# Row copies on SyncE in place of one gather in every eighth chunk of a two-layer relational graph convolution

## The chip, the core and the metric

The kernel runs on one core of a Trainium2 chip. The metric is the device time of one execution in microseconds; the median of three runs is given for the kernel before. Profiles come from one separate execution. PE is TensorE, DVE VectorE, ACT ScalarE, POOL GpSimd and SP SyncE.

## What is computed

There are 50000 nodes with 128 features each and 850000 edges with a source `src`, a target `dst` (sorted) and one of 16 types. The last 50000 edges before sorting are self loops. Cut to what matters:

```python
def layer(h, src, dst, rel, basis, w_comp, loop_w, bias):
    W = einsum('rb,bio->rio', w_comp, basis)              # 16 types from 8 bases
    seg = dst * 16 + rel
    agg = segment_sum(h[src], seg, 50000 * 16).reshape(50000, 16, 128)
    return relu(einsum('nri,rio->no', agg, W) + h @ loop_w + bias)
h = layer(x, ...first weights...)
h = layer(h, ...second weights...)
out = layernorm(x + h)
```

All data are float32. For each edge the row `h[src]` has to be fetched: some 800000 rows of 512 bytes in each layer, since self loops are handled apart.

## The kernel before

**Set-up.** While layer 1 runs, the edge lists are read, self loops are taken out, and the remaining 800000 edges are laid out in 6250 tiles of 128 edges. `rows_of` (L438) puts the source numbers of a tile into a column of `src`, one number on each of 128 partitions, clamped to N - 1. This work is a generator, `later_rows` (L845), of which the chunk loop takes one step per chunk, and more where a chunk would need rows that aren't ready yet.

**Chunks.** A layer is a loop over C = 625 chunks (L940) of K = 10 tiles. For every tile, `gather` (L200 to L204) has POOL issue one indirect transfer: 128 rows of 512 bytes, each from the node that `src` names, into one slot of a ring of GATHERS = 5 buffers of ten slots, fifty in all. The gathers of chunk c + 2 stand in the program at chunk c (L947 to L950). A gather may start when PE has used what was in its slot five chunks ago. Then, for each tile, PE multiplies the gathered rows with `hot`, a matrix of weights and zeros that DVE makes (L869, L876), into `pa` (L974). After five tiles ACT copies `pa` into `aT` (L982). Once per four chunks PE multiplies `aT` by the eight bases (L746), ACT copies the result (L752), PE turns it (L756), and DVE spreads it over slots (L734). PE adds the slots to node sums in `pn` (L788). Beside this run the nodes' own terms (`from_itself`: load of `h_own` L677, L687, L691, eight matmuls and products L702 and L709 and a sum L717 for each group), and `finish` (L805), which adds and stores the result, with a normalisation in layer 2.

**Order.** `beside` (L915) writes by hand which piece of the side work follows which tile. PE, POOL, DVE and ACT keep this order (`manual_schedule`, L861). SP isn't in that list: the order of its transfers is left to the framework's planner. SP issues the loads of edge types `rel` (L617, one for four chunks), `lrel` (L644), `h_own`, `xw` (L787) and the stores (L813, L818). Each engine's queue is in order: an instruction that waits holds up those behind it. Transfers from SP are announced on eight completion lanes that are used in turn, and a transfer is issued only when the one before it on its lane has landed.

**Between the layers.** Layer 2 gathers from H1, which layer 1 writes, so its first gather waits for the last store. `count_up` (L537) then decides whether the assumptions held; if not, `summed` computes everything in another way. With these inputs it is skipped.

Of the kernel before, what the change touches and what calls it, by code (L numbers as in the profile page):

```python
# [39 lines left out]
F32 = mybir.dt.float32  # L40
I32 = mybir.dt.int32
BF16 = mybir.dt.bfloat16
U8 = mybir.dt.uint8
U16 = mybir.dt.uint16
AF = mybir.ActivationFunctionType
OP = mybir.AluOpType
# [4 lines left out]
P = 128  # L51
EPR = 850000
ROW = 10
WN = 12
K = P // WN
S = K * WN
RUN = 672
HALF = K // 2
LIVE = HALF * P
BITS = 6  # L60
LK = 64
LBITS = 10
FETCH = 2
AT = 8
PER = 5
Q = AT // 2
BANK = 512
WEIGHTS = AT * PER * 8
BITS_AT_ONCE = BANK - WEIGHTS - WN
GATHERS = 5  # L70
J = 4
NEAR = 128
BATCH = 4
LAG = BATCH + 2
EPS = 1e-5

# [6 lines left out]
def tile_rgcn_resnorm(  # L83
# [15 lines left out]
    nc = tc.nc  # L99
    N, D = x.shape  # L100
    NR, NB = w_comp1.shape
    E = edges.shape[1] // 3
    R, M = -(-E // RUN), E - N
    C = -(-M // (K * P))
    NG = -(-R // P)
# [3 lines left out]
    ROWS = list(range(0, 2 * C, P)) if 2 * C <= P else [0, *range(P - 8, 2 * C, P)]  # L109
# [4 lines left out]
        end = min(2 * C, ROWS[j + 1] if j + 1 < len(ROWS) else 2 * C) * LIVE  # L114
        return min(NG - 1, -(-(end + LIVE) * E // (M * RUN * P)) - 1) if j else 0

    assert D == P and N >= P and edges.shape[0] == 1 and AT * NR == P and PER * NB * WN <= BANK and AT * PER * NB == WEIGHTS and PER == HALF and S <= P and C >= 4 and M > 0 and N % C == 0 and N % J == 0 and J * D == BANK and C % BATCH == 1 and C > 4 * BATCH and RUN - LK // 2 == LIVE and 2 * C <= NG * P and N <= 1 << 16 and E % ROW == 0
    full, rest = divmod(N, P)
    U = divisor(full, 15)
    assert E < 1 << 24 and 2 * N < 1 << 24  # L120
# [4 lines left out]
    FULL = dram.tile([2 * NP, 2], F32, name="FULL")  # L125

    REL = dram.tile([2 * C, LIVE], U8, name="REL")
    NL = -(-(N + LK) // GN) * GN
    LREL = dram.tile([2 * NL, 1], I32, name="LREL")

# [70 lines left out]
    def gather(to, of, idx):  # L201
        return nc.gpsimd.indirect_dma_start(  # L202
            out=to, out_offset=None, in_=of, in_offset=bass.IndirectOffsetOnAxis(ap=idx, axis=0)
        )  # L204
# [233 lines left out]
    def rows_of(j, pool):  # L438
# [33 lines left out]

        placed = put(srcf, src)

        begin = pool.tile([P, HALF], F32, name="begin")
        tiles = halves[:m, :, 0].rearrange("p (k e) -> p k e", e=P)
        nc.vector.tensor_copy(begin[:m], tiles[:, :, 0])
# [58 lines left out]

    def count_up(pool):  # L537
        last = 5 * NG + len(ROWS)
        off = pool.tile([1, C], F32, name="off_all")
        even = pool.tile([1, C], F32, name="even")  # L540
        nc.gpsimd.iota(
            even,
            pattern=[[N // C, C]],
            base=0,
            channel_multiplier=0,
            allow_small_or_imprecise_dtypes=True,
        )
        nc.vector.tensor_tensor(off, first_of, even, op=OP.subtract)
        for i, (most, op) in enumerate(((-NEAR, OP.is_ge), (NEAR, OP.is_le))):
            nc.vector.scalar_tensor_tensor(  # L550
                even,
                off,
                float(most),
                ones[0:1, 0:1].to_broadcast([1, C]),
                op0=op,
                op1=OP.mult,
                accum_out=picked[0:1, last + i : last + i + 1],
            )
        pick = pool.tile([P, 2], F32, name="pick")
        nc.vector.tensor_reduce(pick[:, 0:1], squares, AX.X, OP.add)  # L560
        nc.vector.tensor_reduce(pick[:, 1:2], picked, AX.X, OP.add)
        total = ps_o.tile([P, BANK], F32, name="po")
        nc.tensor.matmul(total[:1, :2], ones[:, 0:1], pick, start=True, stop=True)
        off = pool.tile([1, 2], F32, name="off2")
        nc.vector.tensor_scalar(off[:, 0:1], total[:1, 0:1], float(N), None, op0=OP.not_equal)
        nc.vector.tensor_scalar(
            off[:, 1:2], total[:1, 1:2], float(E + 2 * NG * (P + 1) + 2 * C), None, op0=OP.not_equal
        )
        nc.vector.tensor_tensor(bad, off[:, 0:1], off[:, 1:2], op=OP.max)
# [19 lines left out]
    def chunked():  # L589
        with (  # L590
# [5 lines left out]
            def ks(c):  # L596
                return min(K, -(-M // P) - c * K)
# [223 lines left out]
            def done(steps):  # L821
                for _ in steps:
                    pass

            loaded, stored = [0], [1]
            rest_of_set_up = set_up(pr)
            next(rest_of_set_up)
# [34 lines left out]
            for n, of in enumerate((x, H1)):  # L862
# [33 lines left out]
                def own_of_all():  # L896

                    for g in range(NGR):
                        while now[0] < min(first(g) + LAG - 5, C - LAG - 2):
                            yield  # L900
                        if n == 0 and g % T == 0:
                            end = min(N, (g + T) * GN)
                            while stored[0] < min(NG, -(-(end + NEAR) * E // (N * RUN * P))):
                                next(coming)
                            loaded[0] = end
                        yield from from_itself(g, of, n)
                        made[0] = g + 1
# [28 lines left out]
                weigh = weights(0, n)  # L936
                next(weigh)
                now, made = [0], [0]
                owning = own_of_all()
                for c in range(C):  # L940
                    now[0] = c
                    if n == 0 and c:

                        next(coming, None)
                        while ready[0] + 1 < len(ROWS) and 2 * min(C, c + FETCH + 5) > ROWS[ready[0] + 1]:
                            next(coming)
                    for to in range(0 if c == 0 else c + FETCH, min(C, c + FETCH + 1)):  # L947
                        buffer = (n * C + to) % GATHERS
                        for k in range(ks(to)):
                            gather(rows[buffer][:, k, :], of, src[:, to * K + k : to * K + k + 1])  # L950
                    g = rows[(n * C + c) % GATHERS]
                    if c == 0:
                        pm = next(weigh)
                        hots[0] = hot_of(0, pm)
                        hots[1] = hot_of(1, pm)
                        if n == 0:
                            done(first_runs)
                    hot = hots.pop(c)
                    if c % BATCH == 0:
                        aTs[c // BATCH] = hp.tile([P, NB, BATCH * S], F32, name="aT")  # L960
                    aT, place_of = aTs[c // BATCH], c % BATCH * S
                    if c >= ALONE + 2:
                        if c == ALONE + 2:
                            done(summing)
                        summing = sum_up(c - 2)
                    elif c % BATCH == 0:
                        summing = slots_of_batch(c - BATCH, aTs[c // BATCH - 1], st, n) if c else iter(())
                    for k in range(0, K, PER):
                        m = min(PER, ks(c) - k)
                        if m > 0:  # L970
                            pa = ps_a.tile([P, BANK], F32, name="pa")
                        for i in range(PER):
                            if i < m:
                                nc.tensor.matmul(  # L974
                                    pa[:, i * NB * WN : (i + 1) * NB * WN],
                                    g[:, k + i, :],
                                    hot[:, k + i].rearrange("e b w -> e (b w)"),
                                    start=True,
                                    stop=True,
                                )  # L980
                            if i == m - 1:
                                nc.scalar.copy(  # L982
                                    aT[:, :, place_of + k * WN : place_of + (k + m) * WN].rearrange(
                                        "d b (i w) -> d i b w", w=WN
                                    ),
                                    pa[:, : m * NB * WN].rearrange("d (i b w) -> d i b w", i=m, w=WN),
                                )
                            beside(k + i, c, owning, summing)
                    if c + 2 < C:
                        if (c + 2) % Q == 0:  # L990
                            pm = next(weigh)
                        hots[c + 2] = hot_of(c + 2, pm)
                        if c + 3 < C and (c + 3) % Q == 0:
                            weigh = weights(c + 3, n)
                            next(weigh)
                    for one in added_in(c + 1) if c + 1 < C else ():
                        masks[one] = masks_of(one)
                    if n == 0 and c == 3:
                        beginning.close()
                    if n == 0 and c == C - 1:  # L1000
                        done(coming)
                        count_up(pr)
# [199 lines left out]
```

## Time and profile before

| | |
|---|---|
| median of 3 runs | 18612.61 us (18609.55 to 18622.79) |
| profiled execution, own time | 18435.78 us |
| its span | 18434.0 us |
| mean granted TensorE clock | 0.762 |
| PE matmuls busy | 11416.0 us (62%) |
| POOL busy | 11894.1 us (65%), 12500 gathers |
| DVE busy | 6704.1 us (36%) |
| ACT busy | 1926.2 us (10%) |
| SP transfers issued | 1000 |
| moved | 1044.31 MB, mean 57 GB/s |

An engine's busy share is the time in which its instructions run, not counting waits and the issuing of transfers on SP. In a group's row, the first figures are its busy time and the mean of one instruction in ns; behind the bar stands how long the engine was idle just before these instructions, and what ended most of that idle time. "issue" means that the profile shows nothing it waited for, and "remote" that the end of the wait isn't on record. A share of busy time averages over stages; what a change is worth has to be read in the stage that it touches.

### The profile page before, as it was taken

The page shows a single profiled execution, that of the slowest core. Times are in us where ns is not written, and L with a number is a line of the kernel's source. Part 1 is how long each engine was busy: PE and PEld are TensorE (multiplying, and loading weights), DVE is VectorE, ACT ScalarE, POOL GpSimd, SP SyncE. Part 2 cuts the span into 40 slices and gives each one's busy share as a digit, 9 for nine tenths or more (in the row PEclk, how much of TensorE's full clock was granted, in tenths as well). Part 3 has the DMA queues.
Part 4 walks back from the last instruction along what each step waited for, and adds up shares of the span by engine and source line. Part 5 has one row for each costly group of instructions (what it writes and reads, how often), then busy time and mean ns, then how long its engine had stood idle before and what let it go on. Part 6 is the DMA issues. An engine that isn't in the chain of part 4 may idle for free. (4 is left out here: it accounts for less than half of the span.)

```text
span 18434.0 us, 136664 instructions
## 1 busy us (share of the span) xinstructions
PE 11416.0 (62%) x45072; PEld 7482.7 (41%) x45072; DVE 6704.1 (36%) x11496; ACT 1926.2 (10%) x3706; POOL 11894.1 (65%) x12533
## 2 busy tenths in 40 slices
PE   4565555656566666666656666666666666666666
PEld 3343333434344444444444444444444444444444
DVE  4344344444333333333333333333333333333333
ACT  0010000101000000010101111111111111111111
POOL 5666666666666666666656666666666666666665
PEclk8777777777777777777777777777777777777777
DMA  2222222222122122221212222222222222222221
GB/s 70 62 60 58 56 58 60 61 59 60 53 54 55 54 54 54 54 54 54 55 49 57 57 57 57 57 57 57 57 57 58 57 57 57 57 57 57 57 57 51
DMA packets 540034, 1044.31 MB, mean 57 GB/s; under 512 B 214689, under 2 KB 259011, under 8 KB 539319
## 3 DMA queue, kind: packets, MB, share of 16 engines
q0 software_dynamic: 403552, 826.82, 17.1%
q1 hardware_dynamic: 132551, 207.21, 3.5%
q8 instruction: 364, 5.96, 0.1%
q14 instruction: 351, 2.88, 0.0%
q10 hardware_dynamic: 3216, 1.45, 0.0%
HBM read 962.30 MB, written 72.31 MB: 56 GB/s over the span
## 5 line engine op out<-in xcount | busy, mean ns | idle before, releaser
L202 POOL DMA_INDIRECT g<-H,src x6250 | 5929.8, 949 | 3090.0 <-issue 1304.3
L202 POOL DMA_INDIRECT g<-in_x_dram,src x6250 | 5938.3, 950 | 3029.0 <-issue 1267.5
L974 PEld LDWEIGHTS pa<-hot,g 128*128 128x128 f32 x25000 | 4547.2, 229 | 6044.9 <-issue 5010.2
L974 PE MATMUL pa<-hot,g 128*128 128x96 f32 x25000 | 4581.9, 308 | 3009.5 <-issue 2081.6
L746 PE MATMUL ps<-aT,basis 128*128 128x480 f32 x4960 | 2910.5, 672 | 707.7 <-ACT aT L982 476.2
L982 ACT COPY aT<-pa 128x480 f32<-128x480 f32 x2500 | 1388.0, 558 | 15113.3 <-remote 8194.1
L788 PE MATMUL pn<-slots,own 120*128 120x512 f32 x4128 | 2553.4, 741 | 615.4 <-DVE slots L734 289.2
L702 PE MATMUL po<-basis,hT 128*128 128x512 f32 x3136 | 2048.6, 741 | 1319.1 <-DVE by L709 1101.2
L709 DVE TENSOR_TENSOR by<-po,lw 128x512 f32<-128x512 f32 x1568 | 1069.5, 687 | 4167.5 <-remote 1469.1
L876 DVE TENSOR_TENSOR hot<-fixed,own 128x960 f32<-128x960 f32 x1250 | 1447.1, 1158 | 2091.2 <-remote 1580.7
L734 DVE TENSOR_TENSOR slots<-po,which 120x512 f32<-120x512 f32 x1240 | 782.6, 683 | 2747.6 <-remote 933.8
L717 DVE TENSOR_REDUCE ls<-by 128x128 f32<-128x1152 f32 (+1 forms) x784 | 1664.2, 2123 | 34.1
L788 PEld LDWEIGHTS pn<-slots,own 120*128 120x128 f32 x4128 | 865.5, 238 | 1202.2 <-issue 687.4
L746 PEld LDWEIGHTS ps<-aT,basis 128*128 128x128 f32 x4960 | 879.1, 221 | 754.3 <-ACT aT L982 494.9
L702 PEld LDWEIGHTS po<-basis,hT 128*128 128x128 f32 x3136 | 563.8, 225 | 1390.6 <-DVE by L709 1151.7
L869 DVE TENSOR_TENSOR own<-fixed,key 128x120 bf16<-128x120 f32 x1250 | 344.5, 276 | 2106.3 <-remote 1040.9
L756 PE MATMUL po<-ident,by_slot 128*120 128x128 f32 x1240 | 317.9, 348 | 1129.2 <-ACT by_slot L752 742.8
L756 PEld LDWEIGHTS po<-ident,by_slot 128*120 128x120 f32 x1240 | 178.3, 181 | 1171.5 <-ACT by_slot L752 770.4
L771 DVE TENSOR_SCALAR own<-col,node 120x128 f32<-120x128 f32 x2064 | 529.4, 296 | 10.4 <-PE pn L788 10.4
L629 PE MATMUL fixed<-each,is_rel 128*128 128x64 f32 x3140 | 457.2, 300 | 8.4 <-DVE is_rel L624 6.1
L629 PEld LDWEIGHTS fixed<-each,is_rel 128*128 128x128 f32 x3140 | 444.1, 221 | 9.4 <-DVE is_rel L624 7.3
L798 PEld LDWEIGHTS pn<-loop,hT 128*128 128x128 f32 x1568 | 234.5, 213 | 134.0 <-issue 133.6
(137 smaller groups left out, 2892.7 us busy)
## 6 DMA issues: line engine op xcount, KB each, us to landing
g<-in_x_dram,src POOLq DMA_INDIRECT x6250
g<-H,src POOLq DMA_INDIRECT x6250
rel<-REL SPq DMA_DIRECT2D x312, 80.0 KB
h_own<-in_x_dram SPq DMA_DIRECT2D x97, 256.0 KB
xw<-in_x_dram SPq DMA_DIRECT2D x97, 256.0 KB
H<-ls SPq DMA_DIRECT2D x97, 256.0 KB
h_own<-H SPq DMA_DIRECT2D x97, 256.0 KB
out_dram<-ls SPq DMA_DIRECT2D x97, 256.0 KB
```

Source lines behind the costliest of these rows:

```text
L202: return nc.gpsimd.indirect_dma_start(out=to, out_offset=None, in_=of, in_offset=bass.IndirectOffsetOnAxis(ap=idx, axis=0))
L629: nc.tensor.matmul(of[:, :, j * NB : (j + 1) * NB], is_rel[:m, j * P : (j + 1) * P], EACH[n][:m], start=True, stop=True,)
L702: nc.tensor.matmul(hb[:m], hT[:, j, :m], BASIS[n][:, b : b + few, :].rearrange("p b d -> p (b d)"), start=True, stop=True,)
L709: nc.vector.tensor_tensor(by[:m, b : b + few, :], hb[:m].rearrange("p (b d) -> p b d", d=D), lw[:m, j, g % T, b : b + few, None].to_broadc ...
L717: nc.vector.tensor_reduce(ls[:m, j, :], by[:m].rearrange("p b d -> p d b"), AX.X, OP.add)
L734: nc.vector.tensor_tensor(st[:k], of[:k, None, :].to_broadcast([k, J, D]), which[:k, c, :, None].to_broadcast([k, J, D]), op=OP.mult,)
L746: nc.tensor.matmul(ps[:, : BATCH * S], BASIS[n][:, b, :], aT[:, b, :], start=b == 0, stop=b == NB - 1)
L771: nc.vector.tensor_scalar(own[:k], col4[:k], node4[:k, c : c + 1], float(-g * GN), op0=OP.subtract, op1=OP.is_equal)
L788: nc.tensor.matmul(sums[g], own, of[:k].rearrange("s j d -> s (j d)"), start=c == first(g), stop=c == final(g),)
L876: nc.vector.tensor_tensor(hot[:, : ks(c)], pm[:, c % Q * K : c % Q * K + ks(c), :, None].to_broadcast([P, ks(c), NB, WN]), own[:, : ks(c), ...
L974: nc.tensor.matmul(pa[:, i * NB * WN : (i + 1) * NB * WN], g[:, k + i, :], hot[:, k + i].rearrange("e b w -> e (b w)"), start=True, stop=True,
L982: nc.scalar.copy(aT[:, :, place_of + k * WN : place_of + (k + m) * WN].rearrange("d b (i w) -> d i b w", w=WN), pa[:, : m * NB * WN].rearr ...
```

## The change

In each layer, chunks 15, 23, 31, ..., 623 get only nine gathers. The tenth tile of such a chunk is brought by SP, row by row: 128 transfers of 512 bytes, each with its address from a register. The registers are loaded, 32 at a time, from a new array ROW_AT in device memory, into which `rows_of` now writes the byte offsets (source number times 512) of the last 128 edges of each half chunk. The rows land in a tile `by_hand` of its own (two buffers) instead of the ring.

The copies for chunk c begin at chunk c - 11 and are spread evenly over the first nine tile steps of eight chunks, so the last is handed out at chunk c - 4. `issue_after` keeps the loads of registers behind the last copy issued. Because offsets are needed earlier, the loop asks for set-up rows eleven chunks sooner. To make room, `count_up` uses two tiles of the set-up in place of its own. ACT copies no rows.

```diff
+BY_HAND = 8
+EARLY = 3
+OFFSETS = 32
...
+    ROW_AT = dram.tile([2 * C, P], I32, name="ROW_AT")
...
+        row_at = pool.tile([P, LIVE], F32, name="real").bitcast(I32)[:, :P]
+        nc.vector.tensor_scalar(row_at[:m], srcf[:m, LIVE - P :], float(N - 1), float(4 * D), op0=OP.min, op1=OP.mult)
+        nc.sync.dma_start(ROW_AT[r0 : r0 + m], row_at[:m])
...
-        off = pool.tile([1, C], F32, name="off_all")
-        even = pool.tile([1, C], F32, name="even")
+        off = pool.tile([P, RUN], F32, name="k_f")[0:1, :C]
+        even = pool.tile([P, RUN], F32, name="loop_f")[0:1, :C]
...
+            def by_hand(c):
+                return ks(c) == K and c >= BY_HAND + EARLY and c % BY_HAND == BY_HAND - 1
+            def row_by_row(c, of):
+                row_at = hp.tile([1, P], I32, name="row_at")
+                nc.sync.dma_start(row_at, ROW_AT[2 * c + 1 : 2 * c + 2])
+                to = hp.tile([P, D], F32, name="by_hand")
+                byte = of.bitcast(U8).rearrange("n d -> (n d)")
+                yield to
+                steps = BY_HAND * (K - 1)
+                for step in range(steps):
+                    for e in range(step * P // steps, (step + 1) * P // steps):
+                        if e % OFFSETS == 0:
+                            with tc.issue_after(behind[-1]) if behind else ExitStack():
+                                _, offsets = nc.values_load_multi_w_load_instructions(
+                                    row_at[:, e : e + OFFSETS],
+                                    engines=[mybir.EngineType.SP],
...
+                        row = to.bitcast(U8)[e : e + 1, :]
+                        behind[:] = [nc.sync.dma_start(row, byte[None, ds(offsets[e % OFFSETS], 4 * D)]).ins]
+                    yield to
...
-                        while ready[0] + 1 < len(ROWS) and 2 * min(C, c + FETCH + 5) > ROWS[ready[0] + 1]:
+                        while ready[0] + 1 < len(ROWS) and 2 * min(C, c + FETCH + 5 + BY_HAND + EARLY) > ROWS[ready[0] + 1]:
...
-                        for k in range(ks(to)):
+                        for k in range(ks(to) - by_hand(to)):
                             gather(rows[buffer][:, k, :], of, src[:, to * K + k : to * K + k + 1])
+                    to = c + BY_HAND + EARLY
+                    if to < C and by_hand(to):
+                        fetching = row_by_row(to, of)
+                        handed[to] = next(fetching)
...
-                                    g[:, k + i, :],
+                                    g[:, k + i, :] if k + i < ks(c) - by_hand(c) else handed.pop(c),
...
+                            if k + i < K - 1:
+                                next(fetching, None)
```

More of the change, by code (lines that the diff above doesn't have):

```diff
@@ L115, in needed @@
         return min(NG - 1, -(-(end + LIVE) * E // (M * RUN * P)) - 1) if j else 0
-    assert D == P and N >= P and edges.shape[0] == 1 and AT * NR == P and PER * NB * WN <= BANK and AT * PER * NB == WEIGHTS and PER == HALF and S <= P and C >= 4 and M > 0 and N % C == 0 and N % J == 0 and J * D == BANK and C % BATCH == 1 and C > 4 * BATCH and RUN - LK // 2 == LIVE and 2 * C <= NG * P and N <= 1 << 16 and E % ROW == 0
+    assert D == P and N >= P and edges.shape[0] == 1 and AT * NR == P and PER * NB * WN <= BANK and AT * PER * NB == WEIGHTS and PER == HALF and S <= P and C >= 4 and M > 0 and N % C == 0 and N % J == 0 and J * D == BANK and C % BATCH == 1 and C > 4 * BATCH and RUN - LK // 2 == LIVE and C <= RUN and 2 * C <= NG * P and N <= 1 << 16 and E % ROW == 0
     full, rest = divmod(N, P)
@@ L823, in done @@
                     pass
+            behind = []
+            def by_hand(c):
[14 more added lines that the diff above has]
+                                    engines=[mybir.EngineType.SP],
+                                    min_val=0,
+                                    max_val=(N - 1) * 4 * D,
+                                    skip_runtime_bounds_check_because="sources are clamped to N - 1, and none is below 0",
+                                )
+                        row = to.bitcast(U8)[e : e + 1, :]
+                        behind[:] = [nc.sync.dma_start(row, byte[None, ds(offsets[e % OFFSETS], 4 * D)]).ins]
+                    yield to
             loaded, stored = [0], [1]
@@ L938, in chunked @@
                 now, made = [0], [0]
+                handed, fetching = {}, iter(())
                 owning = own_of_all()
```

## The prediction, made before the result was known

> **What bounds the kernel now.** I read the page's costliest groups first, then a table by stretches, then a timeline of one stretch. The groups (busy, mean ns | idle before):
>
> ```profile
> L202 POOL DMA_INDIRECT g<-H,src x6250 | 5929.8, 949 | 3090.0 <-issue 1304.3
> L202 POOL DMA_INDIRECT g<-in_x_dram,src x6250 | 5938.3, 950 | 3029.0 <-issue 1267.5
> ...
> L974 PE MATMUL pa<-hot,g 128*128 128x96 f32 x25000 | 4581.9, 308 | 3009.5 <-issue 2081.6
> ```
>
> No engine is full: PE is busy 62% of the span, POOL 65%. A gather is 0.95 us busy, and one that waits for nothing starts 0.30 us after the one before: 1.25 us each, 12.5 us for a chunk of ten. The table shows the real pace (time, POOL busy with number of gathers, granted clock, DMA share, GB/s):
>
> ```profile
> 7000.00:9000.00 2000.00, 1322.59 (x1396) 0.77 0.20 54
> 10000.00:12000.00 2000.00, 1320.61 (x1393) 0.76 0.21 57
> 14000.00:16000.00 2000.00, 1319.93 (x1392) 0.76 0.21 57
> ```
>
> That is 2000/1393 = 1.435 us a gather, 14.35 us a chunk, in both layers: 0.185 us more than the 1.25. In those 0.185 POOL waits for a buffer that PE has not yet freed. Pairing the n-th gather with the n-th pair of L974 matmuls, I find PE taking a row tile 62 us (median; 38 us or more in 99%) after its gather ended. So PE never waits for gathered data once under way; POOL is 42 to 49 gathers ahead and the ring holds 50. By this alone PE would be the bound and gathers would be worth nothing. But PE has no steady pace of its own. Layer 2 starts with an empty ring, so POOL runs without a pause, and the timeline there reads:
>
> ```profile
> 9443.57 0.32 PE L974 MATMUL pa<-hot,g 128*128 128x96 f32 x1 [2.49 <-issue]
> ...
> 9486.98 0.27 ACT L670 COPY lw<-po 128x128 f32<-128x128 f32 x1 [57.69 <-remote]
> ...
> 9493.01 0.95 POOL L202 DMA_INDIRECT g<-H,src  x1 [0.46 <-issue]
> 9497.68 0.56 ACT L982 COPY aT<-pa 128x480 f32<-128x480 f32 x1 [10.43 <-remote]
> 9497.91 0.95 POOL L202 DMA_INDIRECT g<-H,src  x1 [3.95 <-remote]
> 9498.29 0.50 PEld L974 LDWEIGHTS pa<-hot,g 128*128 128x128 f32 x2 [55.84 <-ACT aT L982]
> ```
>
> The matmuls that L670 reads are recorded as done by 9436.3, yet ACT starts 50 us later, and PE, DVE and ACT do nothing meanwhile, while POOL issues gather after gather. When POOL finally has to pause (3.95 us), everything moves at once. The opposite case is the end of layer 1, where the gathers have stopped:
>
> ```profile
> 9437.00:9484.00 47.00, 3.42 (x14) 2.87 (x13) 0.00 (x0) 0.00 (x0) 35.52 (x38) 0.50 0.20 53
> ...
> 9355.00:9395.00 40.00, 38.42 (x219) 27.37 (x217) 22.17 (x40) 6.11 (x11) 1.42 (x2) 1.00 0.04 13
> ```
>
> (columns: PE, PEld, DVE, ACT, POOL, clock, DMA share, GB/s). Without gathers PE is busy 38.42 of 40 us at clock 1.00; the ten aT copies (L982) from 9357.27 to 9395.19 are nine half chunks in 37.92 us, **8.4 us a chunk**. So news of finished matmuls passes slowly while POOL gathers and fast when it pauses; what passes so slowly, I can't name. The time is then gathers x 1.25 us plus the pauses that PE needs.
>
> **The change, part by part.**
>
> *Gathers removed.* Chunks 15, 23, ..., 623 have nine gathers instead of ten: 77 a layer, 154 of 12500. At 1.25 us each: **-192 us**, with the pauses as they are. Upper end: pauses shrink in proportion, 154 x 1.435 = -221. Lower end: two rates. With A = 12500 x 1.25 = 15625 us of gathering and D = 18434 - 15625 = 2809 us without, and 8.4 us a chunk in D (334 chunks), the other 916 of 1250 chunks pass in A, 17.1 us each. With A = 15432, 905 pass in A and 345 need D = 2898: the sum falls by only 104 us. I take 192, since most chunks show POOL at 1.25 throughout and the pause as a short catching up.
>
> *Row copies on SP.* Each tile adds one 512-byte load of offsets, register loads, and 128 one-row copies, 19712 in all. The trace has four one-row copies on SP, static ones (L287): 0.292, 0.246, 0.260, 0.273 us, mean 0.268. Each copy must first see its completion lane free: a semaphore instruction on SP takes 0.017 to 0.028 (medians at L617 and L677). Register loads: the only one (L1160) took 0.475 us for one register. Lower end: four loads a tile, 128 x 0.285 + 1.9 = 38 us. Upper end: one load of 0.475 for each row and one register operation (0.184, L1160): 128 x (0.292 + 0.028 + 0.475 + 0.184) = 125 us. The offsets are bytes already and 32 are asked for at a time, so I take the low rows, 40 to 65 us. The eight lanes allow no more: SP's loads of rel in the trace landed 1.7 to 1.9 us after issue, so eight rows per 1.9 us is 0.24 us a row. The room is eight chunks, 79 x 1.435 = 113 us, of which SP's own issues take 2.8 us (two rel at 0.60, some 1.25 each of h_own, xw and out at 0.33, 0.64 lrel at 0.53). So the copies lie in SP's waiting time, at no cost. Cover: SP is in order, and at 0.86 us a row it is full.
>
> The Trainium skill speaks against this part: "DMA: Bandwidth & Descriptors", section "Rules for kernel authors", says to coalesce many small transfers, since under 64 KB one pays mostly overhead. If its fixed 2 us a DMA (same page, "Anatomy of one DMA", measured for GpSimd) were paid one by one, a tile would take 256 us, by my estimate more than twice the room; the L287 rows, issued 0.35 to 1.1 us apart, say they overlap. "Runtime: NRT & Kernel Launch", section "Instruction fetch mechanics", gives about 200 ns a register for bulk loads; by that estimate a tile takes 62 us, still inside. No run so far shows either price for dynamic copies.
>
> *Who is queued behind them.* SP's next rel (DVE L624 and then PE L629 wait for it), h_own (PE L687), xw and the stores. A copy at one program point waits only for earlier points, and rows are dealt out at 1.8 per tile step, some 0.6 us of SP in each 1.4. Rows of chunk c are all asked for by the end of chunk c-4, so three chunks (43 us) remain to land. Cost taken: nothing.
>
> *PE's wait.* The matmul of the hand-copied tile waits for eight lanes instead of one. A PE semaphore instruction at L974 takes 0.051 us (median): at most 154 x 8 x 0.051 = 63 us, at least 0 behind other work. I take **+20**.
>
> *Set-up.* Ten 128x128 DVE operations (nearest row L771, 120x128, 0.296 us) and ten small stores: **+3**. rows_of is demanded eleven chunks earlier, but counting its steps (one per chunk) it is ready in time either way. count_up's shared buffers are idle by then. Nothing.
>
> **Sum:** -192 + 20 + 3 = -169 us of the profiled 18435.8, or 0.92%. That execution lies 177 us below the median of the runs, so I carry the ratio: 18612.6 x 0.9908 = **18440 us**. Its own range: 221 us saved gives 18390; 104 saved with 66 of cost gives 18574.
>
> **Rivals.**
>
> *PE's chain is the bound anyway (same).* For: the lead of 62 us; the pauses end at PE. Against: the 47 us in which only POOL works. Then POOL just pauses longer: between 18600 and 18640.
>
> *SP fills up (slower).* One mechanism: a dynamic copy costs SP more than its share, the tile lands late, and PE, in order, stands at the chunk's tenth matmul. It decides from (113 - 2.8)/128 = 0.86 us a row. At the upper end, 125 + 2.8 = 128 us per eight chunks against 114.8 now: 154 x 13 = +2000 us, 20600. Near the threshold, or with rel late, a few hundred: 18700 to 18900. For: nothing in the trace shows a copy with an address from a register, and SP's order is not written out by hand. Against: 0.27 us a row.
>
> *Completions slow PE as gathers do (slower).* If it is not POOL's work but the completion messages that hold PE's news back: a gather sends 16 four-byte packets, a row at least one, so (79 x 16 + 128)/(80 x 16) = 1.09 times as many. The A-rate falls to 18.6 us a chunk: 830 chunks in A, 420 x 8.4 = 3528 in D, 18960 profiled, or 19140. Against: xw adds 98 transfers in layer 2 and the pace is unchanged.
>
> **Chances.** Forecast 0.62 (of it 0.02 within 0.2%), PE's chain 0.16, SP 0.14, completions 0.08. Faster by over 0.2% (under 18575): 0.60; within 0.2%, about what a measurement of this kernel can tell from no change: 0.18; slower: 0.22. The range, 18370 to 18900, takes in the forecast, the unchanged case and the mild part of the SP case; it leaves out a full SP and the completions.
>
> **What would show it.** POOL gathers 12346, still 0.95 us; in the steady stretches 8 chunks take 113 us instead of 115, with the gathers' pitch near 1.435. If the pitch grows to 1.453, PE was the bound. SP's copies: about 0.3 us each, 40 to 65 us per tile; if over 0.86, or if PE L974 waits for by_hand, SP is the bound. If ACT's "remote" waits at L982 (8194 us now) grow, completions are to blame. The forecast is wrong if the blocked time of POOL takes back more than half of the 192 us.

## The result

| | before | changed |
|---|---|---|
| median | 18611.08 us (18602.59 to 18622.79, 4 runs) | 18809.44 us (18802.19 to 18828.18, 4 runs) |
| profiled execution | 18435.78 us, span 18434.0 | 18802.19 us, span 18800.3 |
| mean granted clock | 0.762 | 0.758 |

The ratio is 1.0108 (95% interval 1.0090 to 1.0125): the change made the kernel slower, where I had forecast 0.991. The profiled execution of before lies 175 us below its median and that of the changed kernel at its median, so two profiles set side by side show nearly twice the real difference.

One thing must be known ahead of the experiments: the kernel before took 18464 to 18621 us on some of the chips that these runs met and 15803 us on others, so every ratio below is to the kernel before on the same chip, and I call the two kinds of chip A and B (each chip on record was met in one batch of runs only). Within kind A the chips differ by 0.8%, about as much as the effects looked for. The result above is of kind A.

### The profile page after: what moved, and what is told of

It reads as the page before. It is cut to its first block, busy times and chain, and to the rows that moved or that the text cites. A ratio compares the mean times of both kernels' runs of the same rounds, so it can differ in the third digit from the quotient of the medians.

```text
span 18800.3 us, 177030 instructions
## 1 busy us (share of the span) xinstructions
PE 11698.6 (62%) x45072; PEld 7678.2 (41%) x45072; DVE 6710.9 (36%) x11506; ACT 1919.7 (10%) x3706; POOL 11722.7 (62%) x12379
## 5 line engine op out<-in xcount | busy, mean ns | idle before, releaser
L206 POOL DMA_INDIRECT g<-H,src x6173 | 5841.2, 946 | 3351.6 <-issue 1363.6
L206 POOL DMA_INDIRECT g<-in_x_dram,src x6173 | 5855.6, 949 | 3273.2 <-issue 1384.3
L1016 PEld LDWEIGHTS pa<-hot,g 128*128 128x128 f32 x24692 | 4644.3, 238 | 5656.9 <-issue 4927.7
L1016 PE MATMUL pa<-hot,g 128*128 128x96 f32 x24692 | 4690.0, 317 | 2628.5 <-issue 2005.6
L754 PE MATMUL ps<-aT,basis 128*128 128x480 f32 x4960 | 2970.5, 684 | 805.0 <-issue 426.6
L710 PE MATMUL po<-basis,hT 128*128 128x512 f32 x3136 | 2093.6, 756 | 1140.6 <-DVE by L717 774.2
L764 PE MATMUL po<-ident,by_slot 128*120 128x128 f32 x1240 | 374.8, 402 | 1413.2 <-ACT by_slot L760 867.6
L632 DVE TENSOR_SCALAR is_rel<-rel,its_rel 128x640 f32<-128x640 uint8 x314 | 178.5, 568 | 913.8 <-DMA rel<-REL 755.4
```

The source lines that it names most:

```text
L206: return nc.gpsimd.indirect_dma_start(out=to, out_offset=None, in_=of, in_offset=bass.IndirectOffsetOnAxis(ap=idx, axis=0))
L710: nc.tensor.matmul(hb[:m], hT[:, j, :m], BASIS[n][:, b : b + few, :].rearrange("p b d -> p (b d)"), start=True, stop=True,)
L754: nc.tensor.matmul(ps[:, : BATCH * S], BASIS[n][:, b, :], aT[:, b, :], start=b == 0, stop=b == NB - 1)
L764: nc.tensor.transpose(po[:S, q * P : (q + 1) * P], by_slot[:, q * S : (q + 1) * S], ident)
L1016: nc.tensor.matmul(pa[:, i * NB * WN : (i + 1) * NB * WN], g[:, k + i, :] if k + i < ks(c) - by_hand(c) else handed.pop(c), hot[:, k + i]. ...
```

## The profile after

The costliest groups of the changed kernel (busy, mean ns | idle before):

```profile
L206 POOL DMA_INDIRECT g<-H,src x6173 | 5841.2, 946 | 3351.6 <-issue 1363.6
L206 POOL DMA_INDIRECT g<-in_x_dram,src x6173 | 5855.6, 949 | 3273.2 <-issue 1384.3
...
L1016 PE MATMUL pa<-hot,g 128*128 128x96 f32 x24692 | 4690.0, 317 | 2628.5 <-issue 2005.6
```

There are 154 gathers fewer, as long as before, but POOL's idle time ahead of them grew from 6119 to 6625 us. The same three stretches as before (time, POOL busy with number of gathers, granted clock, DMA share, GB/s):

```profile
7000.00:9000.00 2000.00, 1274.52 (x1349) 0.75 0.20 53
10000.00:12000.00 2000.00, 1272.26 (x1346) 0.77 0.21 56
14000.00:16000.00 2000.00, 1275.80 (x1348) 0.76 0.21 56
```

The pitch went from 1.435 to 2000/1347 = 1.485 us, so eight chunks take 79 x 1.485 = 117.3 us; 113 were forecast, and 114.8 is what they took. This is more than the 1.453 that belongs to POOL pausing for just the time that it saved, so something takes longer. The waits of the changed kernel (us in total, times, longest):

```profile
ACT aT L1024 <- remote: 8515.6, 836, 46.6
...
POOL g L206 <- issue: 2747.8, 8715, 4.0
...
POOL g L206 <- remote: 1930.7, 1171, 11.2
...
POOL g L206 <- PE pa L1016: 1382.1, 1649, 7.8
...
DVE is_rel L632 <- DMA rel<-REL: 755.4, 77, 29.4
...
DVE lrel L663 <- DMA lrel<-LREL: 389.1, 47, 26.9
```

and the same waits of the kernel before:

```profile
ACT aT L982 <- remote: 8194.1, 813, 47.8
...
POOL g L202 <- remote: 1822.6, 1379, 6.1
POOL g L202 <- PE pa L974: 1139.3, 1805, 5.8
...
DVE lrel L655 <- DMA lrel<-LREL: 7.5, 3, 3.2
...
DVE is_rel L624 <- DMA rel<-REL: 2.8, 1, 2.8
```

Two things show. The loads of `rel` and `lrel` come late: from the end of their issue to the `is_rel` that uses them were 113.7 us (median) before and are 10.6 now. And ACT's waits at the aT copies, and POOL's for PE, are longer. No PE wait for `by_hand` of any size is there: the last row of a tile is issued 32 us or more (median 60) ahead of its matmul.

What SP does, in a stretch of 30 us (start, length, what, how many in a row):

```profile
14009.91 0.37 SPq L826 DMA_DIRECT2D out_dram<-ls  x1
14010.38 10.62 SPq L859 DMA_DIRECT2D by_hand<-H  x16
14021.01 0.92 SPq L625 DMA_DIRECT2D rel<-REL  x1
14023.46 7.04 SPq L859 DMA_DIRECT2D by_hand<-H  x5
```

Sixteen rows take 10.62 us, 0.66 each, and five more 7.04. An undisturbed row is a register move of 29 ns and an issue of 225 ns (medians), but three in ten of these steps are stretched to 0.70 us or multiples of it. Summed over SP's time, a row takes 0.402 us for its issue, 0.312 for its move and 0.062 for its part of a load of 32 registers (2.05 us, median): 0.776 us. And the framework's order deals rows out in bunches, up to 96 between two loads, with `rel` behind them. That `rel` was late, then, was the first theory (**lateness**). The second was that the copies, being many, slow the passing on of PE's news (**crowding**, my third rival). The third was that **PE's chain** bounds the kernel, so that fewer gathers are worth nothing.

## The experiments

All runs, each with the kernel before on the same chip:

| run | kind | before | this | ratio, 95% |
|---|---|---|---|---|
| e1_nine_no_copies | B | 15802.96 | 15613.07 | 0.9879 (0.9863, 0.9896) |
| e2_ten_and_copies | B | 15802.96 | 15803.61 | 1.0000 (0.9990, 1.0009) |
| e3_rel_on_act | B | 15802.96 | 15604.59 | 0.9872 (0.9856, 0.9889) |
| e4_every_sixteenth | B | 15802.96 | 15709.10 | 0.9940 (0.9923, 0.9957) |
| r1_after_again | A | 18467.86 | 18627.97 | 1.0090 (1.0073, 1.0107) |
| r2_rel_on_act_again | A | 18467.86 | 20444.30 | 1.1071 (1.1053, 1.1090) |
| r3_rel_early_on_sp | A | 18467.86 | 18569.64 | 1.0058 (1.0041, 1.0075) |
| r4_every_fifth_rel_on_act | A | 18467.86 | 24598.55 | 1.3328 (1.3306, 1.3350) |
| s1_nine_no_copies_again | B | 15802.90 | 15613.43 | 0.9880 (0.9863, 0.9896) |
| s2_ten_and_copies_again | B | 15802.90 | 15803.71 | 1.0000 (0.9990, 1.0010) |
| s3_sixteen_rows_a_copy | B | 15802.90 | 15612.30 | 0.9879 (0.9862, 0.9895) |
| s4_static_addresses | B | 15802.90 | 15614.19 | 0.9880 (0.9863, 0.9896) |
| t1_after_third | B | 15803.92 | 15611.77 | 0.9877 (0.9861, 0.9894) |
| t2_nine_no_copies_third | B | 15803.92 | 15609.46 | 0.9877 (0.9860, 0.9893) |
| t3_static_addresses_again | B | 15803.92 | 15615.80 | 0.9881 (0.9864, 0.9897) |
| u1_five_ways_in_turn | A | 18598.21 | 18623.20 | 1.0016 (1.0004, 1.0027) |
| v1_nine_no_copies_whole | A | 18620.84 | 18423.09 | 0.9898 (0.9881, 0.9914) |
| v2_sixteen_rows_whole | A | 18464.40 | 18297.10 | 0.9911 (0.9894, 0.9928) |

### Parts of the change alone, on kind B

**Without copies (e1, repeated as s1, t2 and, on kind A, v1).**

```diff
-                    if to < C and by_hand(to):
-                        fetching = row_by_row(to, of)
-                        handed[to] = next(fetching)
...
-                                    g[:, k + i, :] if k + i < ks(c) - by_hand(c) else handed.pop(c),
+                                    g[:, min(k + i, ks(c) - by_hand(c) - 1), :],
```

> The changed kernel without its row copies: chunks 15, 23, ... have nine gathers, and the matmul of the tenth tile reads the ninth tile's rows again, so one tile in eighty is left out. Lateness (SP's row copies make the loads of rel and lrel late, and DVE waits for them) and crowding (each row copy slows the passing on of PE's news) both expect what the forecast expected of the gathers alone: 18400 to 18450 us, 0.9 to 1.1% below before. If PE's chain sets the pace whatever POOL does, it is 18600 to 18620, as before. The loads of rel are issued some 100 us ahead again in every theory.

**Copies without the gain (e2, repeated as s2).** `for k in range(ks(to) - by_hand(to))` becomes `for k in range(ks(to))`.

> The changed kernel with the tenth gather put back (its rows land in the ring and are not read; PE reads the hand-copied tile). Lateness and crowding: the gathers' price comes on top, 18980 to 19030 us. PE's chain: 18800 to 18820, as changed. Together with the run of nine gathers without copies this gives the price of the copies twice.

**The loads of rel out of SP's queue (e3, r2).** `nc.sync` becomes `nc.scalar` in the loads of `rel` and `lrel`, and `rel` is asked for a chunk earlier:

```diff
+                        if c + 4 < C and (c + 4) % Q == 0:
+                            weigh = weights(c + 4, n)
+                            next(weigh)
                         if c + 3 < C and (c + 3) % Q == 0:
-                            weigh = weights(c + 3, n)
                             next(weigh)
```

> The changed kernel with the loads of rel and lrel issued by ACT instead of SP, rel one chunk before DVE uses it, so that they stand behind no row copy. Lateness: DVE's waits for rel (755 us) and lrel (389 us) fall to under 50 us, and the time to 18430 to 18500 us. Crowding: the waits fall too, but the time stays at 18720 to 18810 us.

**Half as many tiles (e4).** `BY_HAND = 8` becomes 16.

> The changed kernel with one hand-copied tile in sixteen chunks instead of eight (38 a layer), so SP has twice the time for each. Lateness: loads of rel are early again for the most part, and half the gathers' gain shows: 18500 to 18560 us. Crowding: half of everything, gain and price: 18690 to 18730 us.

All four fell on kind B, for which none of these numbers had been written. There the gathers are the plain bound: 190 us less without copies (154 x 1.23), nothing to be seen of copies (e2), half the gain for half the tiles (94 us). So nothing could be told there of a cause that does not exist there. Whether the changed kernel itself gains there, I asked later:

> The changed kernel, untouched, on whichever chip this is. Where the kernel before takes about 15803 us: there copies cost nothing in the other runs, and by lateness as by crowding the ratio is 0.987 to 0.989, faster. Where before takes about 18500 us: 1.009 to 1.011 as twice before.

It does, by 192 us, just the forecast's figure. One stretch of t1, columns as above:

```profile
10000.00:12000.00 2000.00, 1513.50 (x1596) 0.83 0.25 66
```

The pitch is 1.253 us: POOL does not pause. And SP is not disturbed, as its timeline in t1 shows:

```profile
14000.00 3.46 SPq L859 DMA_DIRECT2D by_hand<-H  x11
...
14007.23 4.79 SPq L859 DMA_DIRECT2D by_hand<-H  x15
```

Eleven rows in 3.46 us and fifteen in 4.79: 0.32 us a row, with 0.41 as the mean that counts the loads of registers and waits for lanes. The two batches with repeats told the same, with two further edits, the ones that matter below:

> Nine gathers in the by-hand chunks, no row copies at all; the tenth matmul rereads the ninth gathered tile, so the result is left wrong in one tile of eighty. Where the kernel before takes about 18500 us: if gathers are worth what they last (the forecast's term), 0.990 of it; if PE's chain is the bound and POOL only pauses longer, 0.998 to 1.002. The first leaves the copies to account for 1.9% in the changed kernel, the second for 0.9%. Where before takes about 15803 us: 0.988 again.

> The changed kernel with its tenth gather back, fetched and not read: as many gathers as before, and all row copies. Where before takes about 18500 us: if copies slow the whole (crowding) and gathers are worth 1%, 1.017 to 1.020; if PE's chain is the bound, so that a gather more or less counts nothing, 1.007 to 1.011, as the changed kernel. Where before takes about 15803 us: 1.000 again.

> The changed kernel with 8 copies a tile of 16 neighbouring rows each in place of 128 of one row (the rows are the wrong ones; the same bytes, and registers loaded as before): 1232 copies in place of 19712. SP's load falls to a tenth, so nothing on SP can be late, and there are few issues and completions. Where before takes about 18500 us: if it is the number of copies on SP, late or crowding, that costs, 0.990 to 0.993; if it is their bytes in memory, 1.006 to 1.010 as the changed kernel; if PE's chain is the bound, 0.998 to 1.002. Where before takes about 15803 us: 0.987 to 0.988.

> The changed kernel with all 128 one-row copies of a tile at fixed addresses (the wrong rows, the same number and size): no register is loaded or moved. A row then costs SP its issue alone, 0.3 to 0.5 us in place of 0.78 where before takes about 18500 us. If SP's registers and its fullness do the harm, 0.990 to 0.998; if it is the copies themselves (issue, transfer, completion) that hold up PE's news, 1.006 to 1.010 as the changed kernel. Where before takes about 15803 us: 0.987 to 0.988.

> Nine gathers in the by-hand chunks and no row copies (one tile of eighty rereads another, so the result is left wrong there). Where before takes about 18500 us: 0.990 if gathers are worth what they last, and then the copies cost 1.9% in the changed kernel; 0.998 to 1.002 if PE's chain is the bound, and then the copies cost 0.9%. Where before takes about 15803 us: 0.988.

> 128 one-row copies a tile at fixed addresses (the wrong rows), no register loaded or moved. Where before takes about 18500 us: if SP's registers and its fullness do the harm, half or more of the way from the changed kernel to the one without copies; if the copies themselves (issue, transfer, completion) hold up PE's news, within 0.3% of the changed kernel. Where before takes about 15803 us: 0.988.

In s3 a copy has 16 rows (`if e % 16: continue`, and `16 * 4 * D` bytes from the offset); in s4 the address is `(c * P + e) * 61 % N * 4 * D` in place of a register, and the loads of registers are gone. On kind B both are 0.988, like everything with 154 gathers fewer.

### Is it lateness? On kind A

> The changed kernel, untouched. Where the kernel before takes about 18610 us, 1.011 of it again. Where it takes about 15803 us (POOL gathering almost without a pause, SP's row steps 0.33 us each), lateness and crowding part ways: lateness expects the loads of rel to keep a lead of tens of us there and the kernel to gain what 154 gathers of 1.26 us are worth less little, a ratio of 0.988 to 0.991; crowding (the copies' own cost in the memory or for POOL) expects 0.995 or more, wherever it runs.

> The changed kernel with the loads of rel and lrel issued by ScalarE, rel a chunk earlier, as in e3_rel_on_act. Where the kernel before takes about 18610 us: lateness 0.990 to 0.994 of it, crowding 1.006 to 1.011. Where it takes about 15803 us both expect 0.987 again, and the difference to the untouched changed kernel in this batch is what lateness still costs there: at most 0.2%.

> The changed kernel with rel asked for one chunk earlier and still issued by SyncE behind the copies; lrel stays as it is. If it is lead that the loads lack, a chunk (about 12 to 15 us) brings back most of the gain: where before takes 18610 us, 0.992 to 0.998, left short by lrel, h_own and the stores, which stay late. If the clumps of up to 96 rows (75 us at 0.78 us a row) are longer than the added lead, half or less comes back: 1.000 to 1.008. Where before takes 15803 us: 0.987 to 0.990, as the untouched one.

> A hand-copied tile in every fifth chunk instead of every eighth, rel and lrel on ScalarE: 123 or 124 tiles a layer, 247 gathers fewer than before. Where before takes 15803 us: SP has 49 gathers x 1.264 = 62 us for 128 rows x 0.33 = 42 us, so the copies still fit; 247 x 1.26 = 312 us less, a ratio of 0.980; if copies cost POOL or memory anything beyond SP's time, 0.985 or more. Where before takes 18610 us: a row at 0.78 us needs 100 us of the 70 to 73 there are, SP is full and PE waits for the tile: 1.2 or more by lateness and by crowding.

r1 gave 1.009 again. r3 has the edit of e3 above without the change of engine. The wait of r1 for `rel`, then the waits of r3:

```profile
DVE is_rel L632 <- DMA rel<-REL: 719.2, 81, 43.1
```

```profile
DVE lrel L664 <- DMA lrel<-LREL: 444.9, 48, 33.1
...
DVE is_rel L633 <- DMA rel<-REL: 68.3, 24, 11.3
```

The wait for `rel` is all but gone, and the time fell by 58 us, from 1.0090 to 1.0058 of before. I had expected 0.992 to 0.998 if lateness was the cause, or 1.000 to 1.008 if a chunk's lead was too little. The lead was enough, so **lateness of rel is a small part of the loss and not the cause**. `lrel` is as late as before in r3, and no run moves it alone; at the rate of `rel` (58 us for 651 us of waits) its 445 us would be worth 40 us, by my estimate.

r2 missed by far in the other direction, and both theories with it. The waits of r2, the first row from PE's engine and the second from SP's queue:

```profile
PE po L696 <- DMA h_own<-H: 1523.0, 75, 37.1
PE po L696 <- DMA h_own<-in_x_dram: 1519.8, 73, 52.3
```

```profile
SPq L860 <- DMA rel<-REL: 1749.9, 105, 38.3
SPq L860 <- DMA lrel<-LREL: 394.1, 32, 32.4
```

SP's row copies (L860) now wait for `rel`, which they do not read. The trace's semaphore events say why: ACT's 314 loads of `rel` are announced on the same eight lanes as the rows, and the next copy on such a lane stands until ACT, which is itself held up at its aT copies, has issued its load and the load has landed. A row then takes SP 0.97 us, more than the 0.86 at which I had put the limit, and the loads of `h_own` behind the rows keep PE waiting 3043 us. This is the rival "SP fills up", brought about by the cure. r4 shows it in full: 31744 rows in the span, one per 0.775 us with 0.75 us of SP's time each, and 24599 us in all. Its `rel` is loaded by ACT too, so it is no clean test of that rival: 2190 us of SP's time are again waits for `rel`.

### What the copies cost, way by way

Since I can't choose the kind of chip, one kernel got all the ways in one execution. u1 changes its way every 64 chunks (`mode(c)`), with the edits of e1, s3 and s4 and, for "ten", no tile by hand:

```diff
+            def mode(c):
+                at = (c - (15 if n else 335)) // 64
+                order = ("ten", "none", "dynamic", "fixed", "sixteen", "ten", "none", "dynamic", "fixed") if n else ("sixteen", "none", "dynamic", "ten")
+                return order[at] if 0 <= at < len(order) else "dynamic"
```

> One kernel that changes its way of filling the by-hand tile every 64 chunks (layer 2 from chunk 15: ten gathers and no copies; nine and none, the tenth matmul rereading the ninth tile; nine and dynamic copies, as the changed kernel; nine and 128 copies from fixed addresses; nine and 8 copies of 16 rows; then the first four again; layer 1 from chunk 335: sixteen, none, dynamic, ten). The rows of the fixed and sixteen stretches are the wrong ones, so the result is left wrong. What is read is the time of a chunk in each stretch, on one chip in one execution; the noise of 64 chunks is about 0.1 us. Where the kernel before takes about 18500 us: ten 14.3 to 14.4 us a chunk; none 14.15 to 14.2 if gathers are worth what they last, as ten if PE's chain is the bound; dynamic 14.45 to 14.6; fixed as dynamic if the copies themselves hold up PE's news, 14.2 to 14.35 if SP's registers and fullness do it; sixteen as none if the number of copies counts, as dynamic if their bytes do. Where before takes about 15803 us: ten 12.51, the other four 12.36.

It met kind A. The windows are cut at the aT copy of every 64th chunk of layer 2, from chunk 7 on, eight ahead of a by-hand tile's chunk, since its rows are fetched ahead. The second column is thus the time of 64 chunks, in the order ten, none, dynamic, fixed, sixteen, ten, none, dynamic, fixed:

```profile
9714.50:10646.40 931.90, 608.86 (x642) 0.77 0.21 56
10646.40:11563.20 916.80, 602.07 (x635) 0.77 0.22 57
11563.20:12492.70 929.50, 597.18 (x630) 0.77 0.21 55
12492.70:13421.20 928.50, 601.55 (x634) 0.76 0.22 57
13421.20:14341.00 919.80, 599.04 (x631) 0.77 0.22 57
14341.00:15271.40 930.40, 607.65 (x641) 0.76 0.22 56
15271.40:16186.40 915.00, 598.63 (x632) 0.78 0.22 56
16186.40:17114.30 927.90, 601.03 (x633) 0.77 0.21 56
17114.30:18039.70 925.40, 599.22 (x631) 0.76 0.21 56
```

With the four stretches of layer 1 (sixteen 14.38 us a chunk, none 14.34, dynamic 14.46, ten 14.47), the means are: **ten 14.52, none 14.32, dynamic 14.49, fixed 14.48, sixteen 14.38**. Repeats of one way lie within 0.09 of each other. So a gather less is worth its time here too (0.20 us a chunk, so PE's chain is not the bound), the copies give nearly all of it back (0.17), and it doesn't matter whether their addresses come from registers: copies from fixed addresses cost as much (0.16). Eight copies of 16 rows, the same bytes, cost 0.06, which is within that spread. This speaks for the number of copies, and against SP's registers and the bytes. (It says nothing on lateness: `rel` has a lead of 6 to 21 us, medians, in dynamic and fixed stretches alike, and over 105 in the others. For that there is r3.)

Then the whole kernel on kind A, without copies and with sixteen rows a copy:

> Nine gathers in the by-hand chunks and no row copies in the whole kernel (one tile of eighty rereads another, so the result is left wrong there). By the stretches of u1 (none 14.32 us a chunk, ten 14.52) this kernel takes 0.986 of the time before where before takes about 18500 us; then the copies cost the changed kernel, at 1.009, 2.3%, nearly twice what the stretches give (14.49 to 14.32, 1.2%), and something acts over the whole that the stretches do not show. If instead it takes 0.996 to 0.999, the gathers are worth little in the whole kernel and the copies 1.0 to 1.3%, as in the stretches. Where before takes about 15803 us: 0.988 again.

> The whole kernel with 8 copies a tile of 16 neighbouring rows each in place of 128 of one (the rows are the wrong ones, the bytes the same). Where before takes about 18600 us: by the number of copies, 0.990 to 0.994, since 8 copies a tile should cost a sixteenth of the 2.3 us that 128 cost; by their bytes, 1.005 to 1.010. By the stretches of u1 (sixteen 14.38 us a chunk, none 14.32) 0.994. Where before takes about 15803 us: 0.988 again.

The same stretch of v1, then of v2, to be held against 1393 gathers in the kernel before and 1346 in the changed one:

```profile
10000.00:12000.00 2000.00, 1308.67 (x1379) 0.77 0.22 56
```

```profile
10000.00:12000.00 2000.00, 1310.07 (x1386) 0.77 0.22 57
```

Without copies, and with few, POOL's pauses are short again (r1 has 1363 gathers there; these profiles come from different chips, so the ratios count for more). v1 is 197.8 us faster than before, 0.9898, so the 154 gathers are worth 1.28 us each. v2 is 0.9911, not to be told from v1: 16-row copies cost next to nothing. The pages of the changed kernel and of v2 count the packets:

```profile
DMA packets 576545, 1047.67 MB, mean 56 GB/s; under 512 B 232236, under 2 KB 297674, under 8 KB 575518
```

```profile
DMA packets 576259, 1045.33 MB, mean 57 GB/s; under 512 B 232236, under 2 KB 297674, under 8 KB 575518
```

The packets under 512 B, nearly all of them the four-byte ones that the prediction took for completion messages, are as many in both kernels, and so are those from 512 B to 2 KB, with the rows among them. What v2 has less of is transfers that SP issues, 1232 in place of 19712 (and as many register moves, which made no difference in u1). So what costs here is that SP issues many transfers, with whatever this makes late, and neither their bytes nor their packets.

The changed kernel is 1.009 to 1.011. **The 19712 one-row copies cost it 160 + 198 = 358 us (r1) to 198 + 198 = 396 us (the result): 2.3 to 2.6 us a tile, 18 to 20 ns a copy.** The two terms were measured on different chips, as ratios. In u1's stretches it is only 0.17 x 8 = 1.4 us a tile, so that dynamic copies are no slower there than ten gathers: u1 shows the cost of the copies, but not the loss of 0.9 to 1.1%. Which of the two is off by its noise, or what acts over the whole but not in a stretch, stays open. One difference is on record: DVE waits for `lrel` for 389 us in the changed kernel, 81 us for every 32 tiles, and for 8 us in u1's four stretches of layer 2 with one-row copies, which have 32 tiles.

How do the copies do it? By my count from the trace's semaphore events, while POOL gathers back to back in layer 2, PE's progress is announced 0.74 times a us in the kernel before and 0.70 in v1. In the changed kernel it is 0.75 in the moments without row copies and 0.62 in those with them (r1: 0.71 and 0.65). In v2, counted in the same way, it is 0.71, and in t1, on kind B, 1.26. This fits PE's news passing more slowly while copies run, and POOL's pauses, in which it catches up, getting longer; that the copies act in this way is argued from these counts and not shown by a run of its own. What carries the news, what the two share, and which part of issuing a copy does it, no run shows.

Of the kernels here that leave nothing out, none was faster than the one before on kind A; on kind B the changed kernel is, and rel on ACT (e3) is level with it.

## Why the prediction was wrong, step by step

- **What bounds the kernel**: held as far as the runs test it. Time is gathers x 1.25 us plus the pauses that PE's news needs. On kind B there are no pauses and the gathers alone are the bound.
- **Gathers removed, -192 us**: held on both kinds (-198 in v1, -189 to -194 in e1, s1 and t2). The rival "PE's chain is the bound" is refuted by v1.
- **Row copies on SP at 0.285 us, 40 to 65 us a tile**: mis-sized. Undisturbed they take 0.32 us issue to issue (t1), on kind A 0.776 us of SP's time, 99 us of rows in the 113 us of room. I had read in the trace that news passes slowly while POOL gathers, 50 us without any, and did not ask whether SP's steps would suffer in the same way.
- **"So the copies lie in SP's waiting time, at no cost"**: this is the step that failed. They fit into SP's time, and no tile came late, but their cost is not SP's time: 128 of them lengthen the run by 2.3 to 2.6 us a tile (1.4 in u1's stretches), more than the 1.25 us of the gather that they replace. It shows in POOL's pauses; the way there, slower news from PE, is argued.
- **Who is queued behind them, "nothing"**: wrong, but small. `rel` lost its lead of 114 us; giving back a chunk of lead brought 58 us (r3).
- **PE's wait, +20**: not seen; PE at L1016 hardly ever waits for `by_hand`. **Set-up, +3**: too small for any run here.
- **The rivals**: "completions slow PE as gathers do", to which I gave 0.08, had the right sign and the right signpost (ACT's remote waits grew from 8194 to 8516 us; 8213 in v1, 8756 in r1), but by luck in what it counted: v2 has as many four-byte packets as the changed kernel, and there the copies cost next to nothing. Its size was off as well. With D = 18625 - 15432 = 3193 us in r1, 380 chunks pass in D and 870 in A, 17.7 us each; the kernel before on that chip gives 17.1 and the rival had 18.6. What I held against it, 98 transfers of `xw` in layer 2 that change nothing, was no evidence: the change adds 9856 in a layer. "SP fills up" named the range in which the time fell (18700 to 18900), with the lateness of `rel` as a cause, which accounts for a sixth of the loss that the copies make; SP did fill up in r2 and r4. That the time fell into the range that I had given is luck of this kind too.
- The Trainium skill's rule in "DMA: Bandwidth & Descriptors", section "Rules for kernel authors", that many small transfers are to be coalesced, which I weighed and set aside, points the right way on kind A (v2: 0.991 against 1.009 with the same bytes, though of the wrong rows) and is worth nothing on kind B (s3 0.9879, t1 0.9877). The overhead that it speaks of is not where the time went here: every tile landed in time, and the loss stands in POOL's pauses.
- For a load of registers the Trainium skill, "Runtime: NRT & Kernel Launch", section "Instruction fetch mechanics", gives about 200 ns a register. In the changed kernel's trace a load of 32 took 2.05 us, 0.064 us a register, and the measurement decides.

## What to carry to other kernels

A queue with room for an instruction does not make it free: when a trace shows that something shared is already slow (here 50 us without news of finished work while POOL gathers), price an edit by how often it uses that thing, and hold against it only evidence of the same count. Where the data allow it (scattered rows as here do not), replace many small transfers by few before asking whether their issuing engine has time. And when a cause depends on the chip that is met, put all ways into one execution, in turn, compare stretches, and hold their sum against a run of the whole.

## What the runs showed that I had not expected

- The same kernel takes 15803 us on some chips and 18464 to 18621 us on others; a gather is 0.95 us on both and starts 1.25 us after the last. On the slow kind PE's news and SP's steps come in multiples of 0.70 us while POOL gathers, on the other they don't. What makes the difference, no record here shows (the granted clock differs too, 0.76 and 0.83, but PE is busy for only 62% of the span on the slow kind). The same change is 1.2% faster on the one and 0.9 to 1.1% slower on the other.
- Transfers of SP and ACT share completion lanes. Moving a load from SP to ACT made SP's copies wait 1750 us for that load (r2), and the kernel 10.7% slower.
- One-row copies with the address in a register: a move of 29 ns and an issue of 225 ns, one per 0.32 us undisturbed; a load of 32 registers 2.05 to 2.13 us.
